# A recommender kernel on one core: item tiles of 124 rows in place of 128

## The chip, the core and the metric

The kernel runs on one core of one Trainium2 chip. The core has a matrix engine (TensorE, PE in the profile, with its weight loads as PEld), a vector engine (VectorE, DVE), a scalar engine (ScalarE, ACT), GpSimd (POOL) and a queue engine (SyncE, SP), which run side by side and wait for one another by semaphores. Sixteen DMA engines move data between the device's memory and the core's on-chip memory, which has 128 partitions. The metric is the device time of one execution, in microseconds. A gather, here, is a DMA that POOL issues with a list of row numbers, one for each partition: it fetches one row of a table in memory into each partition.

## The reference, cut to what matters

Inputs: 50001 items, each with two geographic embeddings of 32 values (`E_in`, `E_out`), a history and a target embedding of 64 values, and 32 neighbour items; 16384 users, each with a history of 100 items and a target item.

```python
def _neighbor_attn(E, near_full):                  # E [50001, 32], near_full [50001, 32]
    V = E[near_full]
    scores = jnp.einsum('nd,nkd->nk', E, V) / jnp.sqrt(jnp.float32(GEO_HALF))
    w = jax.nn.softmax(scores, axis=-1)
    return jnp.einsum('nk,nkd->nd', w, V)
...
a_sus = _neighbor_attn(E_in, near_full)
a_inf = _neighbor_attn(E_out, near_full)
hist_bi = jnp.concatenate([a_sus[history], a_inf[history]], axis=-1)
tgt_bi = jnp.concatenate([a_inf[target], a_sus[target]], axis=-1)
h = jnp.concatenate([E_hist[history], hist_bi], axis=-1)
t = jnp.concatenate([E_tgt[target], tgt_bi], axis=-1)
x = h * t[:, None, :]
z = jax.nn.relu(jnp.einsum('bld,hd->blh', x, W1) + b1)
scores = jnp.einsum('blh,h->bl', z, W2[0])
...
```

What follows masks and normalizes the scores over each history, sums to one number `s` over all users, and returns for each user the sigmoid of a cosine between `s` and the target's row `t`.

## The kernel before

The program has two stages, one after the other, both unrolled.

**The item stage** computes the neighbour attention of all items and writes two tables to the device's memory: `table`, with a row of 129 values for each item (the sum of the row, the history embedding, the two attention results), and `ttab`, with the 128 values that a target needs. A tile is 128 items, one to a partition. `NSUB` = 17 tiles make a load of 2176 items, and `NITER` = 23 loads cover the 50001 items; `ROWS` is the padded number, 50048. An item's place is given by the views at lines 99 to 103: load `i`, partition `p`, tile `j` within the load.

For each load, `load` (line 118) brings three tiles from memory on SP's queue: the neighbours' numbers `nidx`, the items' own embeddings `own`, and the history embeddings, straight into their columns of `row`. These have two buffers each, and a load is issued in the middle of the one before it (line 136).

The work goes in batches of `M` = 2 tiles. `gather` (line 131) issues, for each tile and each of the 32 neighbours, one gather on POOL: 128 rows of 64 values (256 B) from `egeo`, in which the two embeddings of an item lie side by side, into the tile `v`. A batch has 64 gathers, and `v` has four buffers. `products` (line 147) waits for a batch's gathers: DVE multiplies `v` with the own embeddings (which ACT has copied to `own_ps`), sums to the scores `sc`, takes the maximum, and ACT makes the exponentials `ex` with their sums `tot`. `attended` (line 182) weighs the neighbours on DVE (`wv`), sums over them and writes the two results into `row`. `finish` (line 206) does, at a load's last tile, the row sum on DVE, a copy on ACT, and the two stores to `ttab` and `table` on ACT's queue (lines 215 and 218); in the last load the last tile is stored by itself.

The order on ACT, DVE and SP is the order in which the program is written (a manual schedule, line 108). The loop at line 225 writes for step `b`: the gathers of batch `b`, `attended` of batch `b - 2`, `products` of batch `b - 1`, `finish` of batch `b - 3`. So on DVE a batch's `products` stands behind the `attended` of the batch before, and POOL may be ahead of both as far as the buffers of `v` allow.

**The user stage** (from line 236) is tiled by 128 users to a partition block. For each user tile and each of the 100 history places POOL gathers 128 rows of `table` (line 302), PE transposes them, DVE multiplies by the targets' rows (line 323), PE multiplies by `W1` (line 335), ACT applies the relu, PE multiplies by `w2` (line 344). The targets' rows come from `ttab` by a gather to each user tile (line 266). Its first gathers read what the item stage's last stores have written.

The outer function pads the inputs to `ROWS` rows: the neighbour lists with the number of the last item, the embeddings with zeros.

Of the kernel before, what the change touches and what calls it, by code (L numbers as in the profile page):

```python
# [10 lines left out]
F32 = mybir.dt.float32  # L11
I32 = mybir.dt.int32
# [6 lines left out]
P = 128  # L19
ITEMS = 50001  # L20
K = 32
G = 32
# [6 lines left out]

NSUB = 17
NITER = -(-ITEMS // (P * NSUB))
ROWS = NITER * P * NSUB

# [8 lines left out]
W = 1 + D  # L46
LAG = 3
M = 2
# [5 lines left out]
def kernel(  # L54
# [21 lines left out]

    table = dram.tile([ROWS, W], F32, name="table")

    ttab = dram.tile([ROWS, D], F32, name="ttab")

# [15 lines left out]


    scale = 1.0 / math.sqrt(G)
    near_v = near.rearrange("(i p j) k -> i p j k", p=P, j=NSUB)
    egeo_v = egeo.rearrange("(i p j) d -> i p j d", p=P, j=NSUB)  # L100
    ehist_v = ehist.rearrange("(i p j) d -> i p j d", p=P, j=NSUB)
    table_v = table.rearrange("(i p j) d -> i p j d", p=P, j=NSUB)
    ttab_v = ttab.rearrange("(i p j) d -> i p j d", p=P, j=NSUB)

    nc.scalar.dma_start(ttab[0 : ITEMS - 1, 0:DE], etgt[0 : ITEMS - 1, :])
    nc.scalar.dma_start(ttab[ITEMS - 1 : ITEMS, 0:DE], etgt[ITEMS - 1 : ITEMS, :])
    with (
        tc.manual_schedule(engines={E.Activation, E.DVE, E.SP}),
        tc.tile_pool(name="n_in", bufs=2) as n_in,
        tc.tile_pool(name="n_v", bufs=4) as n_v,  # L110
        tc.tile_pool(name="n_p", bufs=1) as n_p,
        tc.tile_pool(name="n_s", bufs=3) as n_s,
        tc.tile_pool(name="n_ps", bufs=2, space=bass.MemoryType.PSUM) as n_ps,
    ):
        its = {}
        subs = {}

        def load(it):
            nidx = n_in.tile([P, NSUB, K], I32, name="nidx")
            nc.sync.dma_start(nidx, near_v[it])  # L120
            own = n_in.tile([P, NSUB, 2 * G], F32, name="own")
            nc.sync.dma_start(own, egeo_v[it])

            row = n_in.tile([P, NSUB, W + G], F32, name="row")
            nc.sync.dma_start(row[:, :, 1 : 1 + DE], ehist_v[it])

            its[it] = (nidx, own, row)

        def gather(b):
            v = n_v.tile([P, M, K, 2, G], F32, name="v")
            subs[b]["v"] = v
            for m, s in enumerate(subs[b]["tiles"]):
                it, j = divmod(s, NSUB)
                if j == NSUB // 2 and it + 1 < NITER:
                    load(it + 1)
                nidx = its[it][0]
                for k in range(K):
                    nc.gpsimd.indirect_dma_start(  # L140
                        out=v[:, m, k].rearrange("p t d -> p (t d)"),
                        out_offset=None,
                        in_=egeo,
                        in_offset=bass.IndirectOffsetOnAxis(ap=nidx[:, j, k : k + 1], axis=0),
                    )

        def products(b):
            n = len(subs[b]["tiles"])
            v = subs[b]["v"][:, 0:n]
            own_ps = n_ps.tile([P, M, 1, 2 * G], F32, name="own_ps")  # L150
            for m, s in enumerate(subs[b]["tiles"]):
                it, j = divmod(s, NSUB)
                nc.scalar.copy(own_ps[:, m, 0, :], its[it][1][:, j, :])  # L153
            prod = n_p.tile([P, M, K, 2, G], F32, name="prod")
            nc.vector.tensor_tensor(  # L155
                prod[:, 0:n].rearrange("p m k t d -> p m k (t d)"),
                v.rearrange("p m k t d -> p m k (t d)"),
                own_ps[:, 0:n].to_broadcast([P, n, K, 2 * G]),
                ALU.mult,
            )  # L160
            sc = n_s.tile([P, M, 2, K], F32, name="sc")
            nc.vector.tensor_reduce(  # L162
                sc[:, 0:n].rearrange("p m t k -> p m k t"), prod[:, 0:n], AX.X, ALU.add
            )
            top = n_s.tile([P, M, 2], F32, name="top")
            nc.vector.tensor_reduce(top[:, 0:n], sc[:, 0:n], AX.X, ALU.max)
            nc.vector.tensor_scalar(top[:, 0:n], top[:, 0:n], -scale, None, ALU.mult)
            ex = n_ps.tile([P, M, 2, K], F32, name="ex")
            tot = n_s.tile([P, M, 2, 1], F32, name="tot")
            for m in range(n):  # L170
                for t in range(2):
                    nc.scalar.activation(  # L172
                        ex[:, m, t, :],
                        sc[:, m, t, :],
                        AF.Exp,
                        bias=top[:, m, t : t + 1],
                        scale=scale,
                        accum_out=tot[:, m, t, :],
                    )
            subs[b]["ex"] = (ex, tot)  # L180

        def attended(b):
            n = len(subs[b]["tiles"])
            ex, tot = subs[b]["ex"]
            wv = n_p.tile([P, M, 2, G, K], F32, name="wv")
            for m in range(n):
                for t in range(2):
                    nc.vector.tensor_tensor(  # L188
                        wv[:, m, t].rearrange("p d k -> p k d"),
                        subs[b]["v"][:, m, :, t, :],  # L190
                        ex[:, m, t, :].rearrange("p (k o) -> p k o", o=1).to_broadcast([P, K, G]),
                        ALU.mult,
                    )
            nc.vector.reciprocal(tot[:, 0:n], tot[:, 0:n])
            att = n_s.tile([P, M, 2, G], F32, name="att")
            nc.vector.tensor_reduce(att[:, 0:n], wv[:, 0:n], AX.X, ALU.add)  # L196
            for m, s in enumerate(subs[b]["tiles"]):
                it, j = divmod(s, NSUB)
                nc.vector.tensor_tensor(
                    its[it][2][:, j, 1 + DE : W].rearrange("p (t d) -> p t d", t=2),  # L200
                    att[:, m],
                    tot[:, m].to_broadcast([P, 2, G]),
                    ALU.mult,
                )

        def finish(b):
            for s in subs.pop(b)["tiles"]:
                it, j = divmod(s, NSUB)
                row = its[it][2]
                if j == NSUB - 1 or (it == NITER - 1 and j == NSUB - 2):  # L210
                    j0 = NSUB - 1 if it == NITER - 1 and j == NSUB - 1 else 0
                    js = slice(j0, j + 1)
                    nc.scalar.copy(row[:, js, W : W + G], row[:, js, 1 + DE : 1 + DE + G])
                    nc.vector.tensor_reduce(row[:, js, 0], row[:, js, 1:W], AX.X, ALU.add)
                    nc.scalar.dma_start(
                        ttab_v[it][:, js, DE:D], row[:, js, 1 + DE + G : W + G]
                    )
                    nc.scalar.dma_start(table_v[it][:, js, :], row[:, js, 0:W])
                if j == NSUB - 1:
                    del its[it]  # L220

        NT = NITER * NSUB
        batches = [range(s, min(s + M, NT)) for s in range(0, NT, M)]
        load(0)
        for b in range(len(batches) + 3):
            if b < len(batches):
                subs[b] = {"tiles": batches[b]}
                gather(b)
            if 0 <= b - 2 < len(batches):
                attended(b - 2)  # L230
            if 0 <= b - 1 < len(batches):
                products(b - 1)
            if 0 <= b - 3:
                finish(b - 3)
# [10 lines left out]
    with (  # L245
# [119 lines left out]
        for s in range(last + 2 * LAG + 4):  # L365
            c, g = divmod(s, NG)
            if s < last:
                if g == 0 and c % BSUB == 2 and 0 < c // BSUB and c // BSUB + 1 < UC // BSUB:
                    history_of(c // BSUB + 1)
                if g == 5 and c + 1 < UC:  # L370
                    target_rows(c + 1)
                gather(s)
                turn(s)
                times_target(s)
            if 0 <= s - LAG < last:
                hidden(s - LAG)
            if 0 <= s - 2 * LAG < last:
                scored(s - 2 * LAG)
            if s < last and g == 15 and c + 1 < UC:
                target_work(c + 1)  # L380
            done, left = divmod(s - 2 * LAG - NG, NG)
            if 0 <= done < UC and left == 0:
                weights(done)
            if 0 <= done < UC and left == 2:
                ended(done)
# [87 lines left out]
```

## Time and profile before

| | |
|---|---|
| time, median of 3 runs | 36520.64 us (36513.01 to 36525.43) |
| span of the profiled execution | 36753.4 us |
| first and last gather of the item stage (L140) | 8.6 and 17503.3 us |
| first and last gather of the user stage (L302) | 17536.4 and 36689.4 us |
| POOL busy | 25638.7 us, 25446 instructions |
| gathers of the item stage | 12512 |
| gathers of the user stage, histories and targets | 12800 and 128 |
| loads of `nidx`, of `own`, of `row` | 23 each |

How to read the profile: it is one execution, recorded by the hardware, in microseconds (us). L140 is line 140 of the kernel. A group's line has the busy time and the mean of one instruction, then the idle time of the engine before these instructions, with what ended it; "issue" is time in which the engine waited for nothing that the profile shows. In the table of slices each digit is a busy share in tenths of one fortieth of the span. A timeline's line has the start, the duration, the engine, the line and the operation, with the idle time before it in brackets. POOLq, ACTq and SPq are the queues of the engines, in which DMAs are issued. q0 is the queue of the DMAs that POOL issues, q1 that of SP, q10 that of ACT. A gather's time on POOL is that of issuing it; its data land later. The trace holds the profiled execution alone, and its span is the only time that the page gives of it; the runs of the first row were timed apart.

### The profile page before, as it was taken

To read this page: it belongs to the slowest core of one execution; us is meant where nothing else is said; L and a number is where in the kernel's file an instruction comes from. 1 tells how busy PE (TensorE), PEld (TensorE's weight loads), DVE (VectorE), ACT (ScalarE), POOL (GpSimd) and SP (SyncE) were. 2 spreads that over 40 slices of the span, in tenths; PEclk is the share of its full clock that TensorE was granted. 3 is DMA by queue.
4 is the path that set the end of the run, shared out by engine and by line. 5 is a ranking of instruction groups with operands and counts; after the bars stand their busy time and mean duration, and the time that the engine had idled before them with its cause. 6 is when DMAs were issued, how large, how long until landed. Compare 5 with 4: busy or idle time off the path is not lost. (4 is left out here: it accounts for less than half of the span.)

```text
span 36753.4 us, 140646 instructions
## 1 busy us (share of the span) xinstructions
PE 10978.4 (30%) x44931; PEld 8197.0 (22%) x44931; DVE 6839.7 (19%) x9939; ACT 2598.4 (7%) x5572; POOL 25638.7 (70%) x25446
## 2 busy tenths in 40 slices
PE   0000000000000000000455555555555555555555
PEld 0000000000000000000344444444444444444444
DVE  2222222222222222222111111111111111111111
ACT  0000000000000000000011111111111111111111
POOL 7777777777777777777666666666666666666665
PEclk9999999999999999999766666666666666666666
DMA  1111111111111111111222222222222222222221
GB/s 42 29 27 27 28 27 29 27 27 28 27 29 27 27 28 28 28 27 25 46 45 45 46 45 45 45 46 45 45 45 45 45 46 45 46 45 45 45 45 42
DMA packets 1028095, 1364.65 MB, mean 37 GB/s; under 512 B 559904, under 2 KB 614432, under 8 KB 1027360
## 3 DMA queue, kind: packets, MB, share of 16 engines
q0 software_dynamic: 814080, 1265.42, 16.4%
q10 hardware_dynamic: 151056, 51.51, 0.8%
q1 hardware_dynamic: 62224, 38.72, 0.4%
q8 instruction: 363, 5.95, 0.1%
q14 instruction: 372, 3.05, 0.0%
HBM read 1315.31 MB, written 51.50 MB: 37 GB/s over the span
## 5 line engine op out<-in xcount | busy, mean ns | idle before, releaser
L302 POOL DMA_INDIRECT h<-table,hidx x12800 | 12076.4, 943 | 6922.7 <-issue 3842.1
L140 POOL DMA_INDIRECT v<-in_egeo_dram,nidx x12512 | 13440.9, 1074 | 4062.1 <-issue 3999.8
L344 PEld LDWEIGHTS score<-w_sb,z 128*128 128x128 f32 x25600 | 5127.8, 265 | 7371.6 <-issue 7368.3
L344 PE MATMUL score<-w_sb,z 128*128 128x1 f32 x25600 | 4337.7, 273 | 5275.9 <-issue 5198.2
L278 PE MATMUL hT_ps<-ident,t 128*128 128x128 f32 x128 | 48.6, 380 | 17557.8 <-DMA t<-ttab,tidx 17527.4
L335 PE MATMUL z_ps<-xT,w1T 128*128 128x512 f32 x6400 | 5002.9, 868 | 585.1 <-issue 581.7
L323 DVE TENSOR_TENSOR xT<-hT_ps,tT 128x512 f32<-128x512 f32 x3200 | 2189.8, 688 | 15948.5 <-PE hT_ps L318 7577.8
L278 PEld LDWEIGHTS hT_ps<-ident,t 128*128 128x128 f32 x128 | 35.8, 280 | 17561.6 <-issue 17561.6
L318 PE MATMUL hT_ps<-ident,h 128*128 128x128 f32 x12800 | 3056.8, 360 | 2340.2 <-issue 1889.1
L337 ACT ACTIVATE z<-z_ps,b_sb 128x512 f32<-128x512 f32 x3200 | 2137.4, 686 | 17016.2 <-remote 6414.2
L155 DVE TENSOR_TENSOR prod<-v,own_ps 128x4096 f32<-128x4096 f32 x196 | 864.4, 4410 | 12931.3 <-DMA v<-in_egeo_dram,nidx 12931.3
L318 PEld LDWEIGHTS hT_ps<-ident,h 128*128 128x128 f32 x12800 | 2231.2, 206 | 2730.8 <-issue 2200.1
L335 PEld LDWEIGHTS z_ps<-xT,w1T 128*128 128x128 f32 x6400 | 1440.8, 271 | 876.2 <-issue 875.7
L188 DVE TENSOR_TENSOR wv<-v,ex 128x1024 f32<-128x1024 f32 x782 | 1377.4, 1874 | 315.8 <-ACT ex L172 303.1
L172 ACT ACTIVATE ex<-sc,top 128x32 f32<-128x32 f32 x782 | 227.7, 291 | 16999.8 <-DVE sc L162 10385.7
L162 DVE TENSOR_REDUCE sc<-prod 128x128 f32<-128x4096 f32 x196 | 864.5, 4411 | 6.7
L196 DVE TENSOR_REDUCE att<-wv 128x128 f32<-128x4096 f32 x196 | 864.1, 4409 | 6.0
L326 DVE COPY hsum<-h 128x4 f32<-128x4 f32 x3200 | 537.9, 168 | 0.0
L266 POOL DMA_INDIRECT t<-ttab,tidx x128 | 120.7, 943 | 66.2 <-issue 65.3
L280 DVE COPY tT<-hT_ps 128x128 f32<-128x128 f32 x128 | 37.0, 289 | 593.7 <-remote 343.9
L172 ACT ACTIVATION_READ_ACCUMULATOR ex<-sc,top 128x1 f32 x782 | 146.1, 187 | 0.0
L153 ACT COPY own_ps<-own 128x64 f32<-128x64 f32 x391 | 82.2, 210 | 56.9 <-issue 49.3
(50 smaller groups left out, 638.7 us busy)
## 6 DMA issues: line engine op xcount, KB each, us to landing
h<-table,hidx POOLq DMA_INDIRECT x12800
v<-in_egeo_dram,nidx POOLq DMA_INDIRECT x12512
table<-row ACTq DMA_DIRECT2D x22, 1096.5 KB
own<-in_egeo_dram SPq DMA_DIRECT2D x23, 544.0 KB
row<-in_ehist_dram SPq DMA_DIRECT2D x23, 544.0 KB
ttab<-in_etgt_dram ACTq DMA_DIRECT2D x1, 12500.0 KB
ttab<-row ACTq DMA_DIRECT2D x22, 544.0 KB
hidx<-in_history_dram SPq DMA_DIRECT2D x32, 200.0 KB
```

Of the source, the lines that this page charges most:

```text
L140: nc.gpsimd.indirect_dma_start(out=v[:, m, k].rearrange("p t d -> p (t d)"), out_offset=None, in_=egeo, in_offset=bass.IndirectOffsetOnAxi ...
L155: nc.vector.tensor_tensor(prod[:, 0:n].rearrange("p m k t d -> p m k (t d)"), v.rearrange("p m k t d -> p m k (t d)"), own_ps[:, 0:n].to_b ...
L162: nc.vector.tensor_reduce(sc[:, 0:n].rearrange("p m t k -> p m k t"), prod[:, 0:n], AX.X, ALU.add)
L188: nc.vector.tensor_tensor(wv[:, m, t].rearrange("p d k -> p k d"), subs[b]["v"][:, m, :, t, :], ex[:, m, t, :].rearrange("p (k o) -> p k o ...
L196: nc.vector.tensor_reduce(att[:, 0:n], wv[:, 0:n], AX.X, ALU.add)
L302: nc.gpsimd.indirect_dma_start(out=rows[s][:, q, :], out_offset=None, in_=table, in_offset=bass.IndirectOffsetOnAxis(ap=users[c]["hidx"][: ...
L318: nc.tensor.transpose(hT[s][:, q, :], rows[s][:, q, 1:W], ident)
L323: nc.vector.tensor_tensor(xT[s], hT.pop(s), users[c]["tT"].to_broadcast([D, LG, P]), ALU.mult)
L326: copy = nc.vector.tensor_copy(users[c]["hsum"][:, g * LG : (g + 1) * LG], rows.pop(s)[:, :, 0:1].rearrange("p q o -> p (q o)"),)
L335: nc.tensor.matmul(z_ps, w1T, xT.pop(s), start=True, stop=True)
L337: nc.scalar.activation(z[s], z_ps, AF.Relu, bias=b1_sb)
L344: nc.tensor.matmul(users[c]["score"][:, l : l + 1], of[:, q, :], w2_sb, start=True, stop=True)
```

## The change

A tile of the item stage has `PI` = 124 items in place of `P` = 128, and a load has 15 tiles in place of 17. Every tile of the item stage, and the five views of the tables in memory, get 124 partitions. A load is then 1860 items, `NITER` becomes 27 and `ROWS` 50220. The user stage keeps its 128 partitions and its code.

```diff
-NSUB = 17
-NITER = -(-ITEMS // (P * NSUB))
-ROWS = NITER * P * NSUB
+PI = 124
+NSUB = 15
+NITER = -(-ITEMS // (PI * NSUB))
+ROWS = NITER * PI * NSUB
...
-    near_v = near.rearrange("(i p j) k -> i p j k", p=P, j=NSUB)
+    near_v = near.rearrange("(i p j) k -> i p j k", p=PI, j=NSUB)
...
-    table_v = table.rearrange("(i p j) d -> i p j d", p=P, j=NSUB)
-    ttab_v = ttab.rearrange("(i p j) d -> i p j d", p=P, j=NSUB)
+    table_v = table.rearrange("(i p j) d -> i p j d", p=PI, j=NSUB)
+    ttab_v = ttab.rearrange("(i p j) d -> i p j d", p=PI, j=NSUB)
...
-            nidx = n_in.tile([P, NSUB, K], I32, name="nidx")
+            nidx = n_in.tile([PI, NSUB, K], I32, name="nidx")
             nc.sync.dma_start(nidx, near_v[it])
-            own = n_in.tile([P, NSUB, 2 * G], F32, name="own")
+            own = n_in.tile([PI, NSUB, 2 * G], F32, name="own")
             nc.sync.dma_start(own, egeo_v[it])
 
-            row = n_in.tile([P, NSUB, W + G], F32, name="row")
+            row = n_in.tile([PI, NSUB, W + G], F32, name="row")
             nc.sync.dma_start(row[:, :, 1 : 1 + DE], ehist_v[it])
...
-            v = n_v.tile([P, M, K, 2, G], F32, name="v")
+            v = n_v.tile([PI, M, K, 2, G], F32, name="v")
...
```

The same exchange of `P` for `PI` is made in `own_ps`, `prod`, `sc`, `top`, `ex`, `tot`, `wv` and `att`, and in the three broadcasts of `products` and `attended`.

More of the change, by code (lines that the diff above doesn't have):

```diff
@@ L98 @@
     scale = 1.0 / math.sqrt(G)
-    near_v = near.rearrange("(i p j) k -> i p j k", p=P, j=NSUB)
-    egeo_v = egeo.rearrange("(i p j) d -> i p j d", p=P, j=NSUB)
-    ehist_v = ehist.rearrange("(i p j) d -> i p j d", p=P, j=NSUB)
-    table_v = table.rearrange("(i p j) d -> i p j d", p=P, j=NSUB)
-    ttab_v = ttab.rearrange("(i p j) d -> i p j d", p=P, j=NSUB)
+    near_v = near.rearrange("(i p j) k -> i p j k", p=PI, j=NSUB)
+    egeo_v = egeo.rearrange("(i p j) d -> i p j d", p=PI, j=NSUB)
+    ehist_v = ehist.rearrange("(i p j) d -> i p j d", p=PI, j=NSUB)
+    table_v = table.rearrange("(i p j) d -> i p j d", p=PI, j=NSUB)
+    ttab_v = ttab.rearrange("(i p j) d -> i p j d", p=PI, j=NSUB)
     nc.scalar.dma_start(ttab[0 : ITEMS - 1, 0:DE], etgt[0 : ITEMS - 1, :])
@@ L149, in products @@
             v = subs[b]["v"][:, 0:n]
-            own_ps = n_ps.tile([P, M, 1, 2 * G], F32, name="own_ps")
+            own_ps = n_ps.tile([PI, M, 1, 2 * G], F32, name="own_ps")
             for m, s in enumerate(subs[b]["tiles"]):
@@ L153, in products @@
                 nc.scalar.copy(own_ps[:, m, 0, :], its[it][1][:, j, :])
-            prod = n_p.tile([P, M, K, 2, G], F32, name="prod")
+            prod = n_p.tile([PI, M, K, 2, G], F32, name="prod")
             nc.vector.tensor_tensor(
@@ L157, in products @@
                 v.rearrange("p m k t d -> p m k (t d)"),
-                own_ps[:, 0:n].to_broadcast([P, n, K, 2 * G]),
+                own_ps[:, 0:n].to_broadcast([PI, n, K, 2 * G]),
                 ALU.mult,
             )
-            sc = n_s.tile([P, M, 2, K], F32, name="sc")
+            sc = n_s.tile([PI, M, 2, K], F32, name="sc")
             nc.vector.tensor_reduce(
@@ L164, in products @@
             )
-            top = n_s.tile([P, M, 2], F32, name="top")
+            top = n_s.tile([PI, M, 2], F32, name="top")
             nc.vector.tensor_reduce(top[:, 0:n], sc[:, 0:n], AX.X, ALU.max)
             nc.vector.tensor_scalar(top[:, 0:n], top[:, 0:n], -scale, None, ALU.mult)
-            ex = n_ps.tile([P, M, 2, K], F32, name="ex")
-            tot = n_s.tile([P, M, 2, 1], F32, name="tot")
+            ex = n_ps.tile([PI, M, 2, K], F32, name="ex")
+            tot = n_s.tile([PI, M, 2, 1], F32, name="tot")
             for m in range(n):
@@ L184, in attended @@
             ex, tot = subs[b]["ex"]
-            wv = n_p.tile([P, M, 2, G, K], F32, name="wv")
+            wv = n_p.tile([PI, M, 2, G, K], F32, name="wv")
             for m in range(n):
@@ L190, in attended @@
                         subs[b]["v"][:, m, :, t, :],
-                        ex[:, m, t, :].rearrange("p (k o) -> p k o", o=1).to_broadcast([P, K, G]),
+                        ex[:, m, t, :].rearrange("p (k o) -> p k o", o=1).to_broadcast([PI, K, G]),
                         ALU.mult,
@@ L194, in attended @@
             nc.vector.reciprocal(tot[:, 0:n], tot[:, 0:n])
-            att = n_s.tile([P, M, 2, G], F32, name="att")
+            att = n_s.tile([PI, M, 2, G], F32, name="att")
             nc.vector.tensor_reduce(att[:, 0:n], wv[:, 0:n], AX.X, ALU.add)
@@ L201, in attended @@
                     att[:, m],
-                    tot[:, m].to_broadcast([P, 2, G]),
+                    tot[:, m].to_broadcast([PI, 2, G]),
                     ALU.mult,
```

## The prediction

> **What bounds the kernel now.** I read the page's busy times and its 40 slices first, then two stretches of the table of windows, then the groups by line, then the waits, then the timeline around single gathers.
>
> ```profile
> span 36753.4 us, 140646 instructions
> PE 10978.4 (30%) x44931; PEld 8197.0 (22%) x44931; DVE 6839.7 (19%) x9939; ACT 2598.4 (7%) x5572; POOL 25638.7 (70%) x25446
> ...
> PE   0000000000000000000455555555555555555555
> ...
> POOL 7777777777777777777666666666666666666665
> ...
> DMA  1111111111111111111222222222222222222221
> ```
>
> The slices show two stages. In the first 19 PE does nothing and POOL is at seven tenths: the item stage. From the 20th on PE works and POOL falls to six tenths: the user stage, which the change does not touch. The table of windows (per engine: busy us and instructions, then clock, DMA share, GB/s) makes the same point for one stretch of each:
>
> ```profile
> 3000.00:5000.00 2000.00, 0.00 (x0) 0.00 (x0) 473.66 (x268) 45.59 (x223) 1536.20 (x1427) 1.00 0.15 28
> ...
> 25000.00:36753.00 11753.00, 6734.37 (x27669) 5043.98 (x27667) 1632.88 (x4657) 1354.65 (x2214) 7435.09 (x7881) 0.62 0.20 45
> ```
>
> In 2000 us of the item stage DVE is busy for 474, ACT for 46, the DMA engines for 0.15 of their time, POOL for 1536 in 1427 instructions: one every 1.40 us. The groups by line, and the waits, say what the rest of POOL's time is:
>
> ```profile
> L140 POOL DMA_INDIRECT v<-in_egeo_dram,nidx x12512 | 13440.9, 1074 | 4062.1 <-issue 3999.8 <-DMA v<-in_egeo_dram,nidx 54.9 <-DMA nidx<-in_near_dram 7.3
> L302 POOL DMA_INDIRECT h<-table,hidx x12800 | 12076.4, 943 | 6922.7 <-issue 3842.1 <-PE hT_ps L318 2089.0 <-PE z_ps L335 541.3
> ...
> DVE prod L155 <- DMA v<-in_egeo_dram,nidx: 12931.3, 196, 67.4
> ```
>
> The item stage is POOL issuing gathers one behind the other: 13440.9 busy and 4062.1 idle make 17503.0 us for 12512 gathers, and 3999.8 of the idle time is "issue", waiting for nothing. DVE waits for the gathers (66 us in each of 196 batches), never they for DVE. So the stage lasts as long as the number of gathers times the price of one, 17503.0/12512 = 1.399 us. The bytes hardly enter that price: the user stage's gather at L302 brings rows of 516 B against 256 B here, for 943 ns. Single gathers have several prices:
>
> ```profile
> L140 POOL DMA_INDIRECT v<-in_egeo_dram,nidx x12512: 938/1095/1966, 8.6 to 17503.3; - x199
> L302 POOL DMA_INDIRECT h<-table,hidx x12800: 938/944/1032, 17536.4 to 36689.4; - x197
> ...
> 301.27 1.09 POOL L140 DMA_INDIRECT v<-in_egeo_dram,nidx  x1 [0.30 <-issue]
> ...
> 5009.39 3.60 DVE L188 TENSOR_TENSOR wv<-v,ex 128x1024 f32<-128x1024 f32 x2 [1.82 <-ACT ex L172]
> 5009.49 1.79 POOL L140 DMA_INDIRECT v<-in_egeo_dram,nidx  x1 [0.31 <-issue]
> ...
> 17503.30 0.95 POOL L140 DMA_INDIRECT v<-in_egeo_dram,nidx  x1 [0.30 <-issue]
> ```
>
> The least is 938 ns; the median in the item stage is 1095, beside DVE's L188 1.79 us, and the last ones cost 0.95 again. What sets the 1.09 us level I cannot read from the trace (no engine works in that stretch); it belongs to the stage's mean price and is carried on with it.
>
> **The change, part by part.**
>
> *Number of gathers.* Before: 23 loads x 17 tiles = 391 tiles, times 32 neighbours = 12512. After: a load has 124 x 15 = 1860 items, 50001/1860 needs 27 loads, 405 tiles, 12960 gathers: 448 more (3.6%). At the present price 448 x 1.399 = **+627 us**, all on the path, since POOL is the path.
>
> *Price of a gather of 124 rows.* Every gather of the trace has 128 rows, so this is unknown, and it decides. The added gathers are paid for when 12960 of them save 627 us, 48 ns each. If the floor of 938 ns went purely by rows, four rows fewer would save 938 x 4/128 = 29 ns, 380 us in all. The nearest row on the other side is the dearest gather of 128 rows in the user stage, 1032 against a median of 944: +88 ns, 1140 us in all. In favour of no change at all stands that twice the bytes cost nothing (L302 against L140's floor). I take the present price, 0 ns.
>
> How the rows are dealt to the DMA engines could move the price further:
>
> ```profile
> DMA packets 1028095, 1364.65 MB, mean 37 GB/s; under 512 B 559904, under 2 KB 614432, under 8 KB 1027360
> ...
> q0 software_dynamic: 814080, 1265.42, 16.4%
> q10 hardware_dynamic: 151056, 51.51, 0.8%
> ```
>
> With L266's 128, POOL issues 25440 gathers; 814080/25440 = 32 packets each. Between 2 and 8 KB lie 1027360 - 614432 = 412928 packets, about 16 a gather: one of 8 rows to each engine, and a small one with it. 124 is not divisible by 16: either some engines get 8 rows and one gets 4 (nothing changes for POOL), or equal shares are kept, and the largest number of engines up to 16 that allows it is 4, with 31 rows each. The second is a rival below.
>
> *DVE, ACT.* 405 tiles are 203 batches instead of 196. Per batch DVE works some 30 us:
>
> ```profile
> L155 DVE TENSOR_TENSOR prod<-v,own_ps 128x4096 f32<-128x4096 f32 x195 | 862.1, 4421 | 12910.2 <-DMA v<-in_egeo_dram,nidx 12910.2
> L188 DVE TENSOR_TENSOR wv<-v,ex 128x1024 f32<-128x1024 f32 x782 | 1377.4, 1874 | 315.8 <-ACT ex L172 303.1 <-issue 12.7
> ```
>
> Seven more batches are about 200 us of DVE, hidden under the gathers, of which a batch has 64 x 1.40 = 90 us; without that cover it would be those 200. The elements per partition of each instruction stay, so I leave their durations as they are. The 1.79 us gathers come with DVE's work, so much to a batch, and 64 gathers still make a batch: they are in the mean.
>
> *Loads and stores.* 27 loads, each with three DMAs on SP's queue and two stores on ACT's, for 23. They are issued half a load and more ahead:
>
> ```profile
> 976.74 1.67 ACTq L218 DMA_DIRECT2D table<-row  x1
> 978.46 0.46 ACT L153 COPY own_ps<-own 128x64 f32<-128x64 f32 x2 [2.46 <-issue]
> ...
> 989.53 0.56 SPq L125 DMA_DIRECT2D row<-in_ehist_dram  x1
> ```
>
> L125 on SP's queue waits for the store to free `row`, until some 11 us after its issue at 978.41, and nothing needs the new `row` for most of a load (15 x 32 x 1.40 = 672 us). Behind the stores on ACT's queue stands L153, and behind it DVE's next L155, which has 66 us to spare. Were the stores four times as long, on four engines, 45 us would still fit. Only the ends of the stage show: the first gather waits 7.3 us for `nidx` (L140's row above), and the user stage waits for the last stores:
>
> ```profile
> 17522.37 1.24 ACTq L218 DMA_DIRECT2D table<-row  x1
> 17531.77 0.94 POOL L266 DMA_INDIRECT t<-ttab,tidx  x1 [27.52 <-issue]
> ```
>
> From 17522.37 to 17531.77 are 9.4 us. These two cost nothing more at best and at worst three times 7.3 + 9.4, 50 us; I take the low end, since most of such a short wait is latency, and round it into the sum.
>
> *User stage.* The table has 50220 rows for 50048, with the same 16384 x 100 gathers: 0.
>
> **Sum.** 36753.4 + 627 = 37380 us for a profiled execution. The profiled span stands 233 us (0.6%) above the median of the runs, 36520.6; taking off the same 233 gives 37147, say **37150 us**, 1.7% slower.
>
> A rule that speaks for more than this is in the Trainium skill, "DMA: Bandwidth & Descriptors", section "Why a DMA increments its semaphore by 16 and not by 1": a DMA uses the largest number of engines up to 16 that divides the slowest dimension (its example: 100 partitions, 10 engines), some direct copies from GpSimd excepted, and from GpSimd all 16 engines post to the semaphore. By it 124 rows go to 4 engines, rival B; no row here can show it, as every DMA of the trace with 128 rows divides by 16.
>
> **The rivals.**
>
> *B, fewer packets, faster.* If equal shares are kept on 4 engines, a gather is 31 x 256 = 7936 B on each, two packets of about 4 KB apiece: 8 data packets for 16. If POOL's 944 ns goes by packets (944/32 = 29.5 ns each), 24 cost 708 ns, 236 less. 12960 x 0.236 = 3059 us: 37150 - 3059 = **34090 us**. It decides from 48 ns on, a fifth of this. For it: the price does not follow the bytes, so something counted per gather or per engine must make it up. Against: the 124 rows and the sixteen small packets remain to be written, and those may be what takes the time. A weaker form: the 1.09 us level goes, and every gather costs 944 instead of 1074: 12960 x 0.130 = 1685 us, 35460. The DMA engines, at 0.15 in this stage, would take either.
>
> *C, price by rows.* 29 ns less for each gather: 37150 - 380 = **36770 us**, 0.7% slower. For it: four rows fewer are four addresses fewer to make. Against: no two gathers of the trace differ in rows.
>
> *D, an uneven number of rows costs more.* If shares of 31 rows, or a last short share, cost POOL a slower way, from the +88 ns above: 37150 + 1140 = **38290 us**. If the whole 944 ns went by rows to an engine, 31 for 8, it would be 2.7 us more a gather, some 72000 us; nothing in the rows speaks for that end.
>
> **How the numbers follow.** Chances: the forecast 0.42, B 0.37, C 0.08, D 0.13. The forecast's own range, with C's 29 ns on one side and on the other 21 ns (all gathers at 1095 instead of 1074, 272 us), is 36770 to 37420. The range for 8 in 10 must take in most of B and the near end of D: 34000 to 38300, leaving out the far parts of both. A measurement of this kernel can tell about 0.2% from no change: 73 us, or 6 ns in the price of a gather to either side of 48. So B gives faster 0.36, with 0.03 of all within 0.2%, and the others slower 0.61.
>
> **What would show it.** Right: L140 with 12960 instructions at a mean near 1074 ns and issue gaps of 0.30 us, POOL in the item stage still every 1.40 us, the first L302 near 18165 us instead of 17536, and 32 packets a gather (828416 on q0). Wrong towards B: L140's minimum well under 938, fewer packets on q0 (with 24 for each of these gathers 724736). Wrong towards D: its minimum above 944. Wrong altogether, if POOL's idle time before L140 turns from "issue" to a DMA, or DVE's wait at L155 shrinks to nothing: then a landing or DVE has become the bound.

## The result, and the profile after

The changed kernel takes 39732.9 us (median of 4 runs, 39727.6 to 39751.6) against 36523.0 us for the old one (4 runs, 36513.0 to 36527.8): a ratio of 1.0881, with a 95% interval of 1.0865 to 1.0896. The forecast was 37150 us, with a range of 34000 to 38300: the way was right, slower, but the loss is 3210 us and not 627.

The page of the changed kernel, against the lines of the old one:

```profile
span 39726.4 us, 141355 instructions
PE 10948.7 (28%) x44931; PEld 8091.0 (20%) x44931; DVE 7006.3 (18%) x10027; ACT 2611.6 (7%) x5646; POOL 28971.8 (73%) x25894
...
POOL 8888888888888888888876666666666666666666
...
DMA packets 1249795, 1385.64 MB, mean 35 GB/s; under 512 B 877132, under 2 KB 935180, under 8 KB 1249056
...
q0 software_dynamic: 1035776, 1286.15, 15.1%
```

The item stage now fills 21 slices instead of 19, and POOL is at eight tenths in it: busier, not idler. And q0 has 1035776 packets where the forecast named 828416 for no change in dealing and 724736 for rival B.

The groups by line (busy us and mean ns of one, then idle us before them by releaser) give the size of it:

```profile
L141 POOL DMA_INDIRECT v<-in_egeo_dram,nidx x12960 | 16743.8, 1292 | 3959.4 <-issue 3892.4 <-DMA v<-in_egeo_dram,nidx 57.9 <-DMA nidx<-in_near_dram 9.1
L303 POOL DMA_INDIRECT h<-table,hidx x12800 | 12106.2, 946 | 6667.6 <-issue 3547.5 <-PE hT_ps L319 1604.2 <-PE z_ps L336 775.0
```

The gathers of the item stage (one line further down in the changed kernel) take 16743.8 + 3959.4 = 20703.2 us instead of 17503.0: 3200 more, which is the loss but for 10 us (39732.9 - 36523.0 = 3210). A gather comes every 20703.2/12960 = 1.597 us instead of 1.399. Of the 3200 us, 448 x 1.399 = 627 are the added gathers, and 12960 x (1.5975 - 1.3989) = 2574 their price. The user stage's gather at L303 still has 128 rows and still costs 946 ns.

The distribution (duration in ns, least, median and greatest) and a stretch of the timeline show how the price changed:

```profile
L141 POOL DMA_INDIRECT v<-in_egeo_dram,nidx x12960: 1287/1293/1467, 10.4 to 20703.2; - x200
```

```profile
5029.37 1.29 POOL L141 DMA_INDIRECT v<-in_egeo_dram,nidx  x1 [0.30 <-issue]
...
5031.07 7.05 DVE L189 TENSOR_TENSOR wv<-v,ex 124x1024 f32<-124x1024 f32 x4 [1.82 <-ACT ex L173]
5032.57 1.29 POOL L141 DMA_INDIRECT v<-in_egeo_dram,nidx  x1 [0.31 <-issue]
```

Before, a gather cost 938 to 1966 ns, with a level of 1.09 us and 1.79 us beside DVE's weighted products. Now every one costs 1.29 us, beside the same DVE instruction too. The least price rose by 349 ns, and the spread is gone.

The packets say what POOL does with 124 rows. q0 has 32 packets for each of the 12928 gathers of the user stage (413696); that leaves 622080 for the item stage, 48 a gather instead of 32. Between 2 and 8 KB lie 1249056 - 935180 = 313876 packets; 12928 x 16 = 206848 are the user stage's, 27 x 124 = 3348 those of the `own` loads, which leaves 103680, 8 for each gather. So the data do go to fewer engines, in 8 packets instead of 16, as rival B had it, but the small packets grew from 16 to 40. The trace's packet records of q0, by size in bytes:

```
changed kernel, q0:  4 B x 414208,  60 B x 155520,  64 B x 155520,
                     3840 B x 51840,  4096 B x 53888,  4128 B x 204800
per gather of 124 rows:  4 x 4096 B and 4 x 3840 B  (16 + 15 rows of 256 B on each of 4 engines)
                         12 x 64 B and 12 x 60 B    (16 + 15 entries of 4 B on each of 12 engines)
                         16 x 4 B                   (one for each engine)
```

The records name no engine, so the dealing is read from the sizes: four engines get 31 rows each, and the twelve others get 31 entries of 4 bytes: lists as long as the longest, though they move no rows. That is 31 places on 16 engines where 128 rows took 8. This gave the theory for the experiments: POOL's price is a base and some 13 to 15 ns for each place in that list.

### The profile page after: what moved, and what is told of

Its sections match the earlier page's. It is cut to its first block, busy times and chain, and to the rows that moved or that the text cites. A ratio compares the mean times of both kernels' runs of the same rounds, so it can differ in the third digit from the quotient of the medians.

```text
span 39726.4 us, 141355 instructions
## 1 busy us (share of the span) xinstructions
PE 10948.7 (28%) x44931; PEld 8091.0 (20%) x44931; DVE 7006.3 (18%) x10027; ACT 2611.6 (7%) x5646; POOL 28971.8 (73%) x25894
## 2 busy tenths in 40 slices
DMA packets 1249795, 1385.64 MB, mean 35 GB/s; under 512 B 877132, under 2 KB 935180, under 8 KB 1249056
## 3 DMA queue, kind: packets, MB, share of 16 engines
q0 software_dynamic: 1035776, 1286.15, 15.1%
## 5 line engine op out<-in xcount | busy, mean ns | idle before, releaser
L141 POOL DMA_INDIRECT v<-in_egeo_dram,nidx x12960 | 16743.8, 1292 | 3959.4 <-issue 3892.4
L303 POOL DMA_INDIRECT h<-table,hidx x12800 | 12106.2, 946 | 6667.6 <-issue 3547.5
L345 PEld LDWEIGHTS score<-w_sb,z 128*128 128x128 f32 x25600 | 5041.0, 261 | 6728.5 <-issue 6722.0
L156 DVE TENSOR_TENSOR prod<-v,own_ps 124x4096 f32<-124x4096 f32 x203 | 895.3, 4410 | 15971.2 <-DMA v<-in_egeo_dram,nidx 15971.2
L173 ACT ACTIVATE ex<-sc,top 124x32 f32<-124x32 f32 x810 | 235.9, 291 | 20006.5 <-DVE top L168 19986.9
L189 DVE TENSOR_TENSOR wv<-v,ex 124x1024 f32<-124x1024 f32 x810 | 1428.0, 1872 | 321.3 <-ACT ex L173 321.3
L163 DVE TENSOR_REDUCE sc<-prod 124x128 f32<-124x4096 f32 x203 | 895.4, 4411 | 6.9
L197 DVE TENSOR_REDUCE att<-wv 124x128 f32<-124x4096 f32 x203 | 895.1, 4409 | 6.2
L173 ACT ACTIVATION_READ_ACCUMULATOR ex<-sc,top 124x1 f32 x810 | 151.2, 187 | 0.0
L154 ACT COPY own_ps<-own 124x64 f32<-124x64 f32 x405 | 85.2, 210 | 230.3 <-issue 222.0
```

What stands on the lines that cost most here:

```text
L141: nc.gpsimd.indirect_dma_start(out=v[:, m, k].rearrange("p t d -> p (t d)"), out_offset=None, in_=egeo, in_offset=bass.IndirectOffsetOnAxi ...
L156: nc.vector.tensor_tensor(prod[:, 0:n].rearrange("p m k t d -> p m k (t d)"), v.rearrange("p m k t d -> p m k (t d)"), own_ps[:, 0:n].to_b ...
L163: nc.vector.tensor_reduce(sc[:, 0:n].rearrange("p m t k -> p m k t"), prod[:, 0:n], AX.X, ALU.add)
L189: nc.vector.tensor_tensor(wv[:, m, t].rearrange("p d k -> p k d"), subs[b]["v"][:, m, :, t, :], ex[:, m, t, :].rearrange("p (k o) -> p k o ...
L303: nc.gpsimd.indirect_dma_start(out=rows[s][:, q, :], out_offset=None, in_=table, in_offset=bass.IndirectOffsetOnAxis(ap=users[c]["hidx"][: ...
L345: nc.tensor.matmul(users[c]["score"][:, l : l + 1], of[:, q, :], w2_sb, start=True, stop=True)
```

## The experiments

All kernels below are the changed kernel with the edit shown, or the old one where that is said. n15_128, g128, r126, r125 and r120 ran four times each and the old kernel beside them seven times; all others ran once.

**The count alone (n15_128)**

```diff
-PI = 124
+PI = 128
```

> Tiles of 128 items, but 15 tiles to a load as in the changed kernel: 27 loads, 405 tiles, 12960 gathers of 128 rows. It is the change's added count alone, at the old rows. All theories agree that the gather keeps its old price (mean 1074 ns and 0.325 us of gap), so the item stage is 12960 x 1.399 = 18130 us, 627 more than before, and the time 37150 us. If the time is near 39700 instead, the loss lies in the shorter loads and not in the 124 rows.

37257.3 us against 36545.2 on the same chip, ratio 1.0194 (1.0177 to 1.0211): +712 us.

```profile
L141 POOL DMA_INDIRECT v<-in_egeo_dram,nidx x12960 | 13881.9, 1071 | 4333.6 <-issue 4024.6 <-DMA v<-in_egeo_dram,nidx 301.6 <-DMA nidx<-in_near_dram 7.4
```

The old price came back with the old rows (1071 ns), at the new count. The 85 us over 627 come from idle time: 301.6 us of waiting for earlier gathers to land, against 54.9 before; part of that wait stands in place of issue gaps and of dearer gathers. Most of it (224.9 us) falls after 17600 us, in the last load, most of whose 1920 items are padding that all gather one row.

**The gather's rows alone (g128)**

```diff
-            nidx = n_in.tile([PI, NSUB, K], I32, name="nidx")
-            nc.sync.dma_start(nidx, near_v[it])
+            nidx = n_in.tile([P, NSUB, K], I32, name="nidx")
+            nc.sync.dma_start(nidx[0:PI], near_v[it])
+            nc.sync.dma_start(nidx[PI:P], near_v[0][0 : P - PI])
...
-            v = n_v.tile([PI, M, K, 2, G], F32, name="v")
+            v = n_v.tile([P, M, K, 2, G], F32, name="v")
...
-            v = subs[b]["v"][:, 0:n]
+            v = subs[b]["v"][0:PI, 0:n]
...
```

The same cut to the first `PI` partitions is made where `attended` reads `v`.

> The changed kernel with one part undone: tiles of 124 items, 15 to a load, all loads, stores and arithmetic on 124 partitions, but each gather of the item stage fetches 128 rows, the last four by the numbers of the first items, and nothing reads them. Theory 1 (POOL's price follows the longest list of rows to an engine): 8 rows to each of 16 engines again, price as before (least 938, mean near 1074 ns), time as with 128 items and 15 tiles, 37260 us. Rival: the loads and stores of 124 partitions, or the arithmetic on them, make part of the loss; then the time stays above 37500 us, up to 39730.

37313.8 us against 36675.0 on its chip, ratio 1.0173 (1.0156 to 1.0190): +639 us, the count and no more.

```profile
L142 POOL DMA_INDIRECT v<-in_egeo_dram,nidx x12960: 942/1095/1939, 11.1 to 18132.3; - x200
```

Everything else of the change is in this kernel: loads, stores and arithmetic on 124 partitions, 27 loads. Four rows more in each gather take back the whole 2574 us. The cause is the gather's row count.

**Other row counts (r126, r125, r127, r120, r112, r96)**

```diff
-PI = 124
+PI = 126
```

and likewise 125, 127, 120, 112 and 96. The first three keep 12960 gathers.

> 126 rows, 15 tiles to a load, again 12960 gathers. Theory 1 (slots): POOL writes equally long lists for all 16 engines, and its time is a base plus 15.3 ns for each place in the list, (1292 - 941)/(31 - 8). 126 rows go to 14 engines by 9: 941 + 15 = 956 ns as the least price; the time is 12960 x (0.956 + 0.305) + 19100 = 35450 us if the slower gathers of the old kernel (1.09 and 1.8 us) are gone as in the changed one, and near 37300 us if they are back. Theory 2 (any number of rows that 16 does not divide takes one fixed slower way): 1292 ns and 39730 us. Theory 3 (22 ns for each packet of a gather, 32 before and 48 after): 32 packets, 941 ns.

> 125 rows, 12960 gathers. 125 rows go to 5 engines by 25. Theory 1 (slots): 941 + 17 x 15.3 = 1201 ns, period 1.506, the time 12960 x 1.506 + 19100 = 38620 us. Theory 2 (one fixed slower way): 1292 ns, 39730 us. Theory 3 (packets): 25 x 256 = 6400 B are two packets on each engine, 48 packets, 1292 ns, 39730 us.

> 120 rows, 28 loads of 15 tiles, 420 tiles, 13440 gathers. 120 rows go to 15 engines by 8. Theory 1 (slots): the lists are as long as with 128 rows, least price 941 ns; the time is 13440 x (0.941 + 0.305) + 19100 = 35850 us without the slower gathers of the old kernel and 13440 x 1.399 + 19100 = 37900 us with them. Theory 2 (one fixed slower way): 1292 ns and 13440 x 1.597 + 19100 = 40560 us. Theory 3 (packets): 32 packets, 941 ns.

> 127 rows, 12960 gathers. 127 is divided by no number up to 16 but 1: one engine gets all rows. Theory 1: a straight line through the least prices of 9, 25 and 31 rows to an engine (995, 1205, 1287 ns) rises by 13.3 ns a row; 127 rows make 1287 + 96 x 13.3 = 2560 ns, and the time is 12960 x (2.565 + 0.305) + 19000 = 56200 us. Rival (a slower way with some fixed price for fewer than 14 engines): 1200 to 1300 ns and 38700 to 39800 us.

> 112 rows, 30 loads of 15 tiles, 450 tiles, 14400 gathers. 112 rows go to 16 engines by 7. Theory 1: one place fewer than with 128 rows, least price 938 - 13 = 925 ns; the 1.09 us level comes back, mean near 1070 ns, time 14400 x 1.39 + 19000 = 39000 us. Rival (the price goes by rows): 938 x 112/128 = 821 ns.

> 96 rows, 35 loads of 15 tiles, 525 tiles, 16800 gathers. 96 rows go to 16 engines by 6. Theory 1: least price 938 - 27 = 911 ns, time 16800 x 1.39 + 19000 = 42350 us. Rival (the price goes by rows): 938 x 96/128 = 704 ns, time under 39000 us.

Least, median and greatest ns of the item stage's gather, with 126, 125, 120, 127, 112 and 96 rows in this order, each from its own trace:

```profile
L141 POOL DMA_INDIRECT v<-in_egeo_dram,nidx x12960: 995/1052/2049, 8.3 to 18126.2; - x200
```

```profile
L141 POOL DMA_INDIRECT v<-in_egeo_dram,nidx x12960: 1205/1209/1386, 10.2 to 19628.1; - x200
```

```profile
L141 POOL DMA_INDIRECT v<-in_egeo_dram,nidx x13440: 978/1093/2307, 8.4 to 18801.0; - x198
```

```profile
L141 POOL DMA_INDIRECT v<-in_egeo_dram,nidx x12960: 2545/2552/2726, 18.6 to 37022.9; - x200
```

```profile
L141 POOL DMA_INDIRECT v<-in_egeo_dram,nidx x14400: 929/1095/1917, 8.7 to 20143.7; - x198
```

```profile
L141 POOL DMA_INDIRECT v<-in_egeo_dram,nidx x16800: 916/1095/2090, 9.1 to 23507.2; - x198
```

The period in this table is busy plus idle time of the line, over its count; the old kernel's time is that beside the run. The engines are read from the packet sizes, as above.

| rows | engines x rows | least ns | period us | time us | old kernel, us |
|---|---|---|---|---|---|
| 96 | 16 x 6 | 916 | 1.399 | 42694 | 36675 |
| 112 | 16 x 7 | 929 | 1.399 | 39340 | 36675 |
| 128 (old) | 16 x 8 | 938 | 1.399 | | 36523 |
| 120 | 15 x 8 | 978 | 1.399 | 37857 | 36545 |
| 126 | 14 x 9 | 995 | 1.399 | 37160 | 36545 |
| 125 | 5 x 25 | 1205 | 1.515 | 38679 | 36545 |
| 124 (changed) | 4 x 31 | 1287 | 1.597 | 39733 | 36523 |
| 127 | 1 x 127 | 2545 | 2.857 | 56265 | 36675 |

The least price rises with the rows to an engine, and by one step where fewer than 16 engines have rows. From 9 to 127 places it is a straight line: (2545 - 995)/118 = 13.1 ns a place, and 25 and 31 places lie on it within 4 ns (995 + 16 x 13.1 = 1205, 995 + 22 x 13.1 = 1283). With 16 engines it goes from 916 to 938 in two places, 11 ns each; below 16 engines, 8 rows cost 978 for 938, 40 ns more. The first form of theory 1 had no such step and so missed both runs near it: 956 ns expected for 126 rows and 941 for 120, 995 and 978 measured. What the step is was not tried. As every engine's list is filled to the same length, the longest list and the number of all entries (16 times it) cannot be told apart here. More rows can be cheaper: 126 against 125 and 124. The theory of one fixed slower way for any count that 16 does not divide (1292 ns) fails at 126, 125, 120 and 127. That of a price by packets fails at 125, by the packets of q0:

```profile
q0 software_dynamic: 1035776, 1284.44, 14.7%
```

1035776, to the packet what the changed kernel has, at 1205 ns instead of 1287. The price by rows fails at 112 and 96 (821 and 704 ns expected, 929 and 916 measured).

One column contradicts the old reading of the trace, by which 1.399 us is what POOL takes for a gather. With 96, 112, 120, 126 and 128 rows the period is 1.399 us throughout, though the least price goes from 916 to 995 ns: where the list is shorter, gathers of the 1.09 us level are more (of 1080 to 1110 ns are 43% with 126 rows, 55% with 128 and 58% with 96), and the mean stays.

**Without the attention (nodve, nodve124)**

The old and the changed kernel, each with this in place of `products` and `attended`:

```diff
+        def products(b):
+            v = subs[b]["v"]
+            for m, s in enumerate(subs[b]["tiles"]):
+                it, j = divmod(s, NSUB)
+                nc.vector.tensor_tensor(
+                    its[it][2][:, j, 1 + DE : W].rearrange("p (t d) -> p t d", t=2),
+                    v[:, m, K - 1],
+                    its[it][1][:, j, :].rearrange("p (t d) -> p t d", t=2),
+                    ALU.mult,
+                )
```

> The old kernel (128 items, 17 tiles) with the item stage's attention left out: DVE makes one small product of each tile's last gathered rows, and there are no scores, exponentials and weighted sums. With 96, 112, 120, 126 and 128 rows a gather came every 1.398 us, though the least price ran from 916 to 995 ns, so a second limit holds there. Theory A (the limit comes from DVE's work beside the gathers, the 1.79 us gathers beside the weighted products above all): it goes, gathers cost 0.944 + 0.305 = 1.249 us, the item stage 12512 x 1.249 = 15630 us and the time 34650 us. Theory B (it belongs to the gathers themselves): the period stays 1.398 us and the time near 36500 us.

> The changed kernel (124 items, 15 tiles) with the same attention left out. Theory 1 (POOL's list of 31 places to an engine is the price, and no other engine has a part in it): 1292 ns and a gather every 1.597 us as before, 39730 us. If the time falls by more than 300 us, DVE had a part in the changed kernel's price too.

```profile
L140 POOL DMA_INDIRECT v<-in_egeo_dram,nidx x12512 | 13616.5, 1088 | 3876.6 <-issue 3813.5 <-DMA v<-in_egeo_dram,nidx 55.2 <-DMA nidx<-in_near_dram 8.0
...
L140 POOL DMA_INDIRECT v<-in_egeo_dram,nidx x12512: 940/1095/2495, 9.3 to 17493.3; - x199
```

```profile
L141 POOL DMA_INDIRECT v<-in_egeo_dram,nidx x12960 | 16748.1, 1292 | 3959.4 <-issue 3892.5 <-DMA v<-in_egeo_dram,nidx 57.9 <-DMA nidx<-in_near_dram 8.9
```

36519.9 and 39722.0 us (one run each; the old kernel beside them 36518.0): nothing changes in either. The old kernel's period is 13616.5 + 3876.6 over 12512, 1.398 us, with DVE's work all but gone (130 us busy from 1000 to 17000 us, against 3810 before), so the limit is not DVE's doing: theory B. What DVE's work does change is the spread: in the old kernel's trace 516 gathers take over 1.3 us, in this one 80, while those under 1.0 us go from 36% to 9%. The dear gathers beside DVE's work were made up for by cheap ones, and the mean period stayed. In the changed kernel DVE has no part either.

**A chip without the limit (r117, r119, old128, new124, r117b, r119b)**

117 and 119 rows (`PI = 117`, `PI = 119`) were to tell a limit of 1.398 us from a price.

> 117 rows, 29 loads of 15 tiles, 435 tiles, 13920 gathers. 117 rows go to 9 engines by 13. Theory: a gather takes the longer of a limit of 1.398 us that belongs to gathers as such, and POOL's list, 995 + 13.3 for each place over 9, with 0.305 us of gap. 13 places: least price 995 + 53 = 1048 ns, 1.353 us with the gap, below the limit: the 1.09 us level and the slower gathers are there, mean period 1.398 us, item stage 19460 us. Rival (no limit of 1.398 us; with fewer than 16 engines the list alone sets the price, as at 124 and 125 rows): constant 1048 ns, 1.353 us, 18830 us.

> 119 rows, again 29 loads, 13920 gathers. 119 rows go to 7 engines by 17. Theory: the list takes 995 + 8 x 13.3 = 1101 ns, 1.406 us with the gap, just above the limit of 1.398: all gathers near 1101 ns, no level of 1.09 us and hardly a slower one, mean period 1.406 us, item stage 19570 us. Rival (slower gathers come on top of the list's price): a mean some 130 ns above the least price, period over 1.5 us.

They ran on a chip on which the old kernel takes 31861 us, not 36520, and so did not tell it: 34372 and 35872 us. (The expectation dealt 117 rows wrongly: 13 divides 117, and its q0 has 13 packets of 2304 B a gather, 9 rows to each of 13 engines.) So they were run again together with the two kernels themselves, unchanged (old128, new124), and that chip too was of the second kind.

> The old kernel, unchanged, for its profile on the chip on which the next three run. Two kinds of chip were met: on most the old kernel takes 36520 us, on one 31860. Theory (a gather takes the longer of POOL's list with its gap, 0.940 + 0.305 us, and a limit of 1.398 us that belongs to the chip's condition): on the first kind the period is 1.398 us with the 1.09 us level; on the second 1.247 us, constant, and the item stage 15600 us.

> The changed kernel, unchanged, on the same chip. Theory: its list of 31 places with the gap, 1.597 us, is above the limit, so its item stage is 20700 us on either kind of chip. On the first kind the time is 39730 us, 8.8% over the old kernel's; on the second 20700 + 16200 = 36900 us, 15.8% over it. Rival (the list itself is quicker on the second kind): under 36000 us there.

> 117 rows, dealt to 13 engines by 9, as in the run before (13 divides 117, which its expectation overlooked). Theory: least price 992 ns as there; period 1.398 us on the first kind of chip, 1.303 us on the second. Rival (with fewer than 16 engines the list alone sets the price on any chip): 1.303 us on the first kind too.

> 119 rows, 7 engines by 17. Theory: 1098 + 305 ns is 1.403 us, just above the limit of 1.398, so the period is 1.40 to 1.41 us on either kind of chip, with hardly a gather at 1.2 or 1.8 us. Rival (slower gathers come on top of the list's price on the first kind): mean over 1.2 us, period over 1.5 us.

31858, 36899, 34329 and 35908 us. The groups of the old and the changed kernel there:

```profile
L140 POOL DMA_INDIRECT v<-in_egeo_dram,nidx x12512 | 11804.1, 943 | 3854.7 <-issue 3757.5 <-DMA v<-in_egeo_dram,nidx 89.5 <-DMA nidx<-in_near_dram 7.7
```

```profile
L141 POOL DMA_INDIRECT v<-in_egeo_dram,nidx x12960 | 16722.9, 1290 | 3956.3 <-issue 3888.6 <-DMA v<-in_egeo_dram,nidx 58.5 <-DMA nidx<-in_near_dram 9.2
```

And the distributions, of the old kernel and of 117 and 119 rows:

```profile
L140 POOL DMA_INDIRECT v<-in_egeo_dram,nidx x12512: 938/944/1097, 9.1 to 15659.2; - x199
```

```profile
L141 POOL DMA_INDIRECT v<-in_egeo_dram,nidx x13920: 992/997/1171, 8.5 to 18116.0; - x199
```

```profile
L141 POOL DMA_INDIRECT v<-in_egeo_dram,nidx x13920: 1098/1103/1277, 9.0 to 19689.1; - x199
```

On this chip the old kernel's gathers cost 944 ns with hardly an exception, beside all of DVE's work, and come every (11804.1 + 3854.7)/12512 = 1.252 us. The changed kernel's cost what they cost elsewhere, 1290 ns and 1.596 us. 117 rows with 9 places have 992 ns and a period of 1.301 us; 126 rows, also 9 places, had 995 ns and 1.399 us on the first kind of chip. 119 rows with 17 places cost 1098 ns; the line says 995 + 8 x 13.1 = 1100. So on the first kind of chip a gather takes the longer of two things, POOL's list with its gap and 1.398 us, and the change had to pass the second before its price showed: the least list rose by 349 ns, the period by 199. Without the limit the change costs 36899 - 31858 = 5040 us, 15.8% (one run each). That 117 and 119 rows meet the limit on the first kind of chip was not tried there.

No version in these runs beats the old kernel: 128 rows are the most that a gather has had here, and the list is at its shortest for its rows.

## Why the prediction was wrong

**What bounds the kernel** was read right as far as it went: POOL's gathers, one behind the other, with DVE and ACT covered. The page of the changed kernel has the same shape, and nodve and nodve124 show the cover directly. That the 1.399 us of the old kernel is a limit, and not POOL's own time for a list of 8, could not be read from its trace. The 30 us of DVE a batch were too many: 473.66 us in the 2000 us shown, which hold about 22 batches, are some 21 us; it cost nothing, as the seven added batches (167 us more of DVE, 7006.3 - 6839.7) stayed covered.

**The number of gathers** was right, 627 us: 639 measured by g128, 712 by n15_128 with its load of padding.

**The price of 124 rows** is the step that failed: "I take the present price, 0 ns". It rose by 199 ns in the period, 2574 us, four fifths of the loss. The dealing was named, 31 rows to each of 4 engines, but the term was set by the bytes, whose cost had been seen to be nothing, and by the rows, of which there were fewer. The price follows neither; it follows the longest list to one engine, which went from 8 to 31. No row of the old trace had another list than 8, so the size was not to be had from it. What could be had from it is that the length of the list was an unknown, open on the dear side; the range closed that side with +88 ns, from the spread of gathers whose lists were all alike. Of the prediction's signs of being wrong, the one towards D came: a minimum above 944, with 1287. POOL's idle time stayed "issue" (3892.4 of 3959.4 us).

The Trainium skill's rule on the number of engines ("DMA: Bandwidth & Descriptors", section "Why a DMA increments its semaphore by 16 and not by 1") agrees with the trace in its dealing: the 8 data packets a gather make 4 shares of 31 rows, and by the packet sizes 126 rows make 14 shares of 9 (2304 B), 125 rows 5 of 25 and 127 rows one of 127.

**Rival B** had the dealing right and the sign wrong. It took fewer data packets for less work; the small ones grew by 24, and packets are not what is paid (r125). **Rival D**, that shares of 31 rows cost POOL more time, was nearest to the mechanism, at a chance of 0.13; its size was short: 88 ns against 349 in the least price, 218 in the mean, and its far end of 2.7 us assumed that all 944 ns go by the list, when 8 places are 8 x 13 = 105 of them. **Rival C** fell: four rows fewer saved nothing.

**The 1.09 us level** was carried on as part of a mean price. It was a limit, met with 96, 112, 120, 126 and 128 rows and gone with 124, 125 and 127, where the list with its gap is longer than 1.398 us. Carried on as it was, it did no harm to the count; with the 349 ns of the longer list added to the old mean, it would have made the price 1.75 us instead of 1.597.

**Loads and stores** cost little, as said. The end of the stage in the changed kernel:

```profile
20703.25 1.29 POOL L141 DMA_INDIRECT v<-in_egeo_dram,nidx  x1 [0.30 <-issue]
...
20721.13 10.99 ACTq L216 DMA_DIRECT2D ttab<-row  x1
20732.16 1.20 ACTq L219 DMA_DIRECT2D table<-row  x1
...
20737.96 0.96 POOL L267 DMA_INDIRECT t<-ttab,tidx  x1 [33.42 <-DMA table<-row]
20739.95 0.96 POOL L303 DMA_INDIRECT h<-table,hidx  x1 [1.02 <-DMA hidx<-in_history_dram]
```

From the last gather to the first of the user stage are 36.7 us, against 33.1 before; the issue of the last store to `ttab` took 10.99 us. The first gather starts at 10.4 us instead of 8.6. Together 5 us, within the 0 to 50 given.

**The user stage** was to stay. In the two profiled executions it is 231 us shorter after the change (39726.4 - 20740.0 against 36753.4 - 17536.4), which is by how much the old kernel's profiled execution lay above its median; the changed kernel's lies within 7 us of its own. Between the medians the difference is the item stage's alone.

## What to carry to other kernels

Before changing the partitions of a gather, work out how its rows are dealt to the 16 DMA engines: POOL pays for the longest list on any engine, 13 ns a place here, and a count just under 128 can be far dearer than 128 (127 rows: 2545 ns). Change it in multiples of 16, and expect little from fewer rows, since 96 cost 916 ns. And where an instruction has two price levels in one trace, run it with less to do: if the total stays, it is a limit and not a price.

## What the runs showed of the hardware that was not expected

- By the sizes of its packets, an indirect gather from POOL gives every one of the 16 DMA engines a list as long as the longest, with entries of 4 B where it has no rows: 12 x 31 of them in each gather of 124 rows.
- On the chips of most runs POOL's gathers came no faster than one every 1.398 us, with 96, 112, 120, 126 and 128 rows and with or without DVE's work. On two other chips the old kernel took 31860 instead of 36520 us, and in its profile on one of them a gather came every 1.252 us. The limit does not hold from the start: in the old kernel's first batches gathers cost 944 ns. What it is stays open. The rows of a gather with their bytes (96 to 128 rows), and DVE's and ACT's work on the attention, do not set it. A queue of gathers still to land does not show either: by the packet records the last packet of a gather ends about 1.18 us after POOL is done with it on both kinds of chip (medians of the old kernel's gathers 2000 to 12000), before POOL is done with the next one.

```profile
L140 POOL DMA_INDIRECT v<-in_egeo_dram,nidx x65 | 61.3, 944 | 19.8 <-issue 19.8
```

This is the old kernel's group in the stretch from 100 to 180 us on the first kind of chip.

- The limit of the item stage is not all that tells the two kinds of chip apart. Of the 4897 us between the two profiles of the old kernel (36753.4 - 31856.5), the user stage has 3051, more than the item stage: 31856.5 - 15690.1 = 16166 us against 19217, at a lower granted TensorE clock (0.51 from 17000 to 31000 us, against 0.62 from 20000 to 36000). Its gathers cost POOL 944 ns there too; POOL's idle time before them is 3901.7 us against 6922.7. Why is not known.
